# Making the first image's queries, keys and values beside the second image's Mamba tiles

## The chip, the cores and the metric

The kernel runs on one core of a Trainium2 chip. The metric is the time on the device in microseconds (us). Before the change it is 4571.91 us, the median of three runs (4563.61, 4571.91 and 4572.27); the execution that was profiled took 4562.89 us and its profile spans 4561.0 us. The core has five engines that work at the same time, each through its own instructions in their order: PE (matrix products), DVE (vector work), ACT (activation functions, also copies), POOL (general work, here elementwise products) and SP, which here only issues transfers (DMA).

## The reference

Two images of 256 channels by 4096 positions (64 x 64) pass through two layers, each added to its own input. Cut to what matters:

```
# layer 0, on groupnorm(x): a Mamba block and an MLP, per image
yn  = layernorm(y) * gamma + beta
xm, z = split(yn @ W_in.T)                     # 512 channels each
u   = silu(causal_conv4(xm) + conv_b)
dt  = softplus(W_dt @ (W_xp @ u)[:16] + b_dt)  # B, C: the other 2 x 16 rows
h   = exp(dt * A) * h + (dt * u) * B           # one step per position, 16 states per channel
ym  = (sum(h * C) + u * D) * silu(z)
y2  = ym @ W_out.T + yn
x   = x + gelu(y2 @ W1.T + b1) @ W2.T + b2 + y2

# layer 1, on groupnorm(x): attention, 8 heads of 32 channels over 4096 positions
q, k, v = split(groupnorm(x) @ qkv_w.T + qkv_b)
x   = x + softmax(q.T @ k / sqrt(32)) @ v
```

Layer 1 of an image needs the whole of layer 0 of that image, since its group norm takes means over all positions; it needs nothing of the other image.

## The kernel before

**Stages.** The program is `mamba_stage` for both images, then `attention_block` for image 0, then for image 1. Positions are cut into tiles of 512, so an image has 8 tiles and the Mamba stage 16, image 0 first.

**The Mamba stage.** A tile is worked in 32 steps: 4 groups of 128 channels times 4 groups of states times 2 halves. In each step ACT makes two decays `da` (L725), PE spreads a row of B over the partitions (`bn`, L418), POOL and DVE multiply it with dt * u (`dbu` and `bn`, L731), DVE runs two scans (L736) into a tile `h`, POOL multiplies `h` by C (L742), and PE sums over the states into `y` (L768). Around the steps of a tile lie its `front` (load, norms, convolution, softplus; POOL takes part with L587, L588 and L590) and its `back`: the product with W_out (L614), and the MLP, whose 8 blocks of hidden values go through PE, ACT's gelu (L639) and PE again (L650). Its end adds the input, takes statistics for layer 1's group norm (L660 and L661) and stores the tile to a scratch in memory (L664).

**What sets the order.** The order in each engine is not written by hand: every operation is added to a `Plan` with an engine, a due time counted in steps, a cost in us, what it reads and writes, and for transfers a time to land. `Plan.order` then runs these through in planned time and gives each engine the ready operation with the earliest due time; the result is the order in which instructions are issued, and the chip follows that order per engine whatever the real times are. So an instruction that waits holds all that stands behind it on its engine. For a transfer the planner counts mostly 0.8 us of SP and 2 to 5 us of landing (3.0 for stores of 512 KB). Buffers are rings of the same planner: `mm` has 3 PSUM banks for all products but `bn` and `y`, `bn` 2, `h` 5, `yn` 3, and `hid`, the 8 blocks of the MLP's hidden values, is one buffer (16 KB in each partition). A tile's MLP can only begin to fill it when the tile before has read it.

**Attention of an image.** `prepare` loads the weights w_qkv, takes the group norm's scales, and for each of 8 tiles loads x, normalises (L894), makes keys and queries (L904) as two halves each, a rounded high one (L914, ACT) and the rest (L915, DVE), stores both to memory (L918), makes values (L927, L934) into the buffer `v`, and loads keys back in the layout of the heads (L823). Then the main loop takes 512 slots of one block of 128 keys for 4 heads: logits on PE (L987), exponentials on ACT (L1000), products with v on PE (L1021) and sums of the exponentials on DVE and POOL (L1013, L1051 to L1054). In its first tiles it also stores `v` to memory, 128 transfers in all, for a fallback that only runs if a value has gone out of range.

Of the kernel before, what the change touches and what calls it, by code (L numbers as in the profile page):

```python
# [11 lines left out]
F32 = mybir.dt.float32  # L12
F32R = mybir.dt.float32r
AF = mybir.ActivationFunctionType
ALU = mybir.AluOpType
# [4 lines left out]
P = 128  # L20
T = 512
# [4 lines left out]
KG = HEADS * D // P  # L26
# [215 lines left out]
SWITCH = 6  # L242
HORIZON = 24


@with_exitstack
def mamba_stage(ctx, tc, xs, stats_out, consts, w, outs):

# [23 lines left out]
    KH = HID // P  # L272
# [8 lines left out]
    wp = ctx.enter_context(tc.tile_pool(name="l0w", bufs=1))  # L281
# [7 lines left out]
    mm = ring("mm", 3, pool=ps, free=True)  # L289
# [10 lines left out]
    r_hid, r_xb = ring("hid", 1, KH), ring("x_back", 1, KC)  # L300
# [3 lines left out]
    add = plan.add  # L304

    def image_tile(x, t):
        return x.rearrange("(k p) l -> p k l", p=P)[:, :, bass.ts(t, T)]


    stats_in = [wp.tile([P, KC, NT, nc.vector.BN_STATS_DIM], F32, name=f"stats_in{b}") for b in range(IMAGES)]  # L310
    stats_bufs = [Buf(parts=KC * NT, tile=s) for s in stats_in]

    def first(b, t, due):
        xt = Buf(r_h)
# [68 lines left out]
    for row in (0, LOW):  # L383
        rows = slice(row, row + R)
# [14 lines left out]
    late_buf = Buf()  # L399

    def load_late():
        for tile_, name in ((w_out, "W_outT"), (w_1, "W1T"), (w_2, "W2T")):
            nc.sync.dma_start(tile_, w[name].rearrange("(k p) f -> p k f", p=P))

# [5 lines left out]
    nc.vector.memset(halo, 0.0)  # L410
    state_buf = Buf(parts=IMAGES * KD * QUAD * NQ, tile=state)
    halo_buf = Buf(parts=IMAGES * KD, tile=halo)
    scales = wp.tile([P, IMAGES, KC, 2], F32, name="scales")
    scales_buf = Buf(parts=IMAGES * KC, tile=scales)

    def matmul(out, pairs):
        for i, (lhsT, rhs) in enumerate(pairs):
# [2 lines left out]
    def group_norm(b, k, due):  # L420

        s = Buf(r_gn)
        p1, p2 = Buf(mm), Buf(mm)
        out = scales_buf[b * KC + k]

        def aggregate():
            nc.vector.bn_aggr(s.tile[:, 0:2], stats_in[b][:, k, :, :].rearrange("p a s -> p (a s)"))

        def spread():


            nc.vector.tensor_copy(s.tile[:, 2:3], p1.tile[:, 0:1])
            nc.vector.tensor_sub(s.tile[:, 3:4], s.tile[:, 0:1], s.tile[:, 2:3])
            nc.vector.scalar_tensor_tensor(
                s.tile[:, 4:5], s.tile[:, 3:4], s.tile[:, 3:4], s.tile[:, 1:2], ALU.mult, ALU.add
            )

        def root():
            nc.scalar.activation(s.tile[:, 5:6], p2.tile[:, 0:1], AF.Ln, bias=eps_t)
# [12 lines left out]
        add("DVE", due, 0.2, shift, [s], [out])  # L452
# [8 lines left out]
    STEPS = KD * NQ * 2  # L461
# [142 lines left out]
    def back(i):  # L604

        b, t = divmod(i, NT)
        d = tiles[i]
        due = (i + 1) * STEPS + 3
        yn = d.yn
        for m in range(KC):  # L610
            po = Buf(mm)

            def project(k, po=po, m=m):
                nc.tensor.matmul(  # L614
                    po.tile, lhsT=w_out[:, k, bass.ts(m, P)], rhs=d.z[k].tile, start=(k == 0), stop=(k == KD - 1)
                )
# [12 lines left out]
        hid = Buf(r_hid, KH)  # L629
        xt = Buf(r_xb, KC)  # L630
        add("SP", due + 6, 0.8, lambda: nc.sync.dma_start(xt.tile, image_tile(xs[b], t)), [], [xt], lands=4.0)
        for f in range(KH):
            ph = Buf(mm)

            def up(f=f, ph=ph):
                matmul(ph.tile, [(w_1[:, c, bass.ts(f, P)], yn.tile[:, c, :]) for c in range(KC)])

            def gelu(f=f, ph=ph):
                nc.scalar.activation(hid.tile[:, f, :], ph.tile, AF.Gelu, bias=b_1[:, f : f + 1])  # L639

            add("PE", due + 5 + 1.5 * f, 1.9, up, [yn], [ph, hid] if f == 0 else [ph])
            add("ACT", due + 6 + 1.5 * f, 0.7, gelu, [ph], [hid[f]], ("gelu",))
        for m in range(KC):
            acc = Buf(mm)

            def down(f, acc=acc, m=m):
                if f == 0:
                    nc.tensor.matmul(acc.tile, lhsT=ident, rhs=yn.tile[:, m, :], start=True, stop=False)
                for f in (f, f + 1):
                    nc.tensor.matmul(  # L650
                        acc.tile, lhsT=w_2[:, f, bass.ts(m, P)], rhs=hid.tile[:, f, :], start=False, stop=(f == KH - 1)
                    )

            for f in range(0, KH, 2):
                reads = [hid, yn[m]] if f == 0 else [hid[f], hid[f + 1]]
                add("PE", due + 19 + 4 * m + f / 2, 2.7 if f == 0 else 1.8, lambda f=f, down=down: down(f), reads, [acc])

            def end(m=m, acc=acc):
                x = xt.tile[:, m, :]
                nc.vector.scalar_tensor_tensor(x, acc.tile, b_2[:, m : m + 1], x, ALU.add, ALU.add)  # L660
                nc.vector.bn_stats(stats_out[b][:, m, t, :], x)  # L661

            add("DVE", due + 24 + 4 * m, 1.45, end, [acc], [xt[m]])
        add("SP", due + 29, 0.8, lambda: nc.sync.dma_start(image_tile(outs[b], t), xt.tile), [xt], [], lands=3.0)  # L664


    class Step:
# [120 lines left out]
    for i, d in enumerate(tiles):  # L788
        d.z, d.b, d.c, d.dt_rep, d.dtu_rep = [], [], [], {}, {}
        if i + 1 < len(tiles):  # L790
            front(i + 1)
        for k in range(KD):
            gate(d, k, i * STEPS + 8 * k - 1)
            for g in range(NQ * 2):
                step(i * STEPS + k * NQ * 2 + g)
        back(i)
    with tc.manual_schedule():
        plan.issue()

# [27 lines left out]


@with_exitstack
def attention_block(ctx, tc, b, stats, consts, w, out, scratch, range_t):  # L830

# [4 lines left out]
    nc = tc.nc  # L836
    ident, gmat, _, eps_t = consts
# [113 lines left out]
                        load_keys(0, t - 1)  # L951
                load_keys(0, NT - 1)

    prepare()

    p1 = ctx.enter_context(tc.tile_pool(name=f"l1p1{b}", bufs=1))
    p3 = ctx.enter_context(tc.tile_pool(name=f"l1p3{b}", bufs=2))
# [133 lines left out]
    with tc.manual_schedule():  # L1091
        logits(0, 0)
        logits(0, 1)
        s = 0
        while s <= S or side.waiting:
            i, c = divmod(s, NC)
            if s < S:
                if c == 0:
                    tiles[i] = Slot()
                    load_queries(i + 1)  # L1100
                if i % NT == NT - 1 and i < KG * NT - 1 and c % (T // P) == 0:

                    load_keys(i // NT + 1, c * P // T)
                exponentials(s, 0)
                exponentials(s, 1)
            if 1 <= i <= KG:
                nc.sync.dma_start(scratch.v[b * KG + i - 1, :, c, :], v[:, c, (i - 1) * P : i * P])
            if 0 < s <= S:
                values(s - 1)
                if c == 0:  # L1110
                    side.start(side.now, finish(i - 1))
            side.run()
            logits(s + 1, 0)
            logits(s + 1, 1)
            if s < S:
                add_up(s)
            s += 1
# [100 lines left out]
def conv_preact_kernel(ctx: ExitStack, tc: tile.TileContext, x: bass.AP, w: dict, out: bass.AP):  # L1218
# [16 lines left out]
    scratch = Scratch(ctx.enter_context(tc.tile_pool(name="scratch", bufs=1, space=DRAM)), B * KG, L)  # L1235
    range_t = const.tile([P, 2, B * KG * NT], F32, name="range_t")
    stats1 = [const.tile([P, KC, NT, nc.vector.BN_STATS_DIM], F32, name=f"stats1{b}") for b in range(B)]
    mamba_stage(tc, [x[b] for b in range(B)], stats1, consts, w, [scratch.image(b) for b in range(B)])
    for b in range(B):
        attention_block(tc, b, stats1[b], consts, w, out[b], scratch, range_t)  # L1240
    flag = out_of_range(tc, range_t)
    with tc.If(flag > 0):
        attention_any_range(tc, consts, w, out, scratch)
# [51 lines left out]
```

## Time and profile before

| stage | from, us | to, us | what is seen |
|---|---|---|---|
| Mamba, steps of 16 tiles | start | 2024 | POOL 119.0 us of every 120, DVE 112, ACT 100, DMA 0.36 of its time |
| end of the last tile | 2024 | 2068 | PE nearly alone: W_out, the MLP |
| preparation of image 0 | 2068 | 2171 | PE 91 of 101 us, DMA 0.88, POOL 0 |
| attention of image 0 | 2171 | 3312 | PE, ACT, DVE and POOL all busy |
| preparation of image 1 | 3312 | 3413 | as for image 0 |
| attention of image 1 | 3413 | 4561 | as for image 0 |

| engine | busy us | share of the span |
|---|---|---|
| PE | 4266.7 | 94% |
| DVE | 3945.2 | 86% |
| POOL | 3816.1 | 84% |
| ACT | 3747.0 | 82% |

How to read it: busy time of the whole span mixes stages with different limits, so each stage has to be looked at by itself. PE's busy time counts matmuls that overlap from start to end, and an instruction can be counted busy while the next is already in the array. A row of the profile names the line, the engine, the tile that is written and the tiles that are read, the number of instructions, the busy time and the mean of one, and then the idle time of the engine just before them and what ended it. A line such as L418 is a helper for several products: there the tiles tell which.

### The profile page before, as it was taken

The numbers are of one execution on the slowest core, as the hardware profiler recorded it, in microseconds if no ns is written. First come the engines' busy times: TensorE is split into PE (matmuls) and PEld (weight loads), VectorE is DVE, ScalarE is ACT, GpSimd is POOL, SyncE is SP. The second block draws the span as 40 slices with busy tenths as digits, with TensorE's granted clock in tenths as the row PEclk, the third lists the DMA queues.
The fourth block names the chain that finished last, engine by engine and source line by source line (L and its number), as shares of the span: only waits on it lengthen the run. The fifth ranks groups of instructions, "written<-read, shape, count | busy, mean of one in ns | idle before, by whom it ended". The sixth has DMA issues, their size and how long they took to land. (4 is left out here: it accounts for less than half of the span.)

```text
span 4561.0 us, 53981 instructions
## 1 busy us (share of the span) xinstructions
PE 4266.7 (94%) x18530; PEld 1640.5 (36%) x18530; DVE 3945.2 (86%) x3340; ACT 3747.0 (82%) x4801; POOL 3816.1 (84%) x2251
## 2 busy tenths in 40 slices
PE   5889999999999999888999999999989999999998
PEld 2233333333333333324333333333343333333333
DVE  4999999999999999963789898898948898898988
ACT  4788888888888888751999999999829999999997
POOL 2999999999999999970788888888808888888887
PEclk9899999999999999989999999999999999999999
DMA  5233333333333333317220140101082101401000
GB/s 190 99 120 121 105 104 121 121 125 125 125 125 114 118 123 123 103 51 233 77 55 17 26 94 24 27 17 26 10 265 54 45 17 26 102 17 26 25 23 8
DMA packets 162315, 379.54 MB, mean 83 GB/s; under 512 B 23409, under 2 KB 41585, under 8 KB 153841
## 3 DMA queue, kind: packets, MB, share of 16 engines
q1 hardware_dynamic: 162032, 376.03, 26.9%
q8 instruction: 147, 2.41, 0.2%
q14 instruction: 136, 1.11, 0.1%
HBM read 282.64 MB, written 93.32 MB: 82 GB/s over the span
## 5 line engine op out<-in xcount | busy, mean ns | idle before, releaser
L1013 DVE TENSOR_REDUCE chunk<-chunk 128x1024 f32<-128x4096 f32 x288 | 1269.8, 4409 | 209.4 <-ACT chunk L1000 209.4
L1000 ACT ACTIVATE chunk<-s 128x1024 f32<-128x1024 f32 x992 | 1118.3, 1127 | 180.9 <-PE s L987 139.3
L1054 POOL TENSOR_TENSOR acc_p<-acc_p,e 128x1024 f32<-128x1024 f32 x480 | 1152.1, 2400 | 136.0 <-ACT e L1000 117.3
L987 PE MATMUL s<-q,k 128*128 128x512 f32 x4096 | 1224.8, 420 | 3.6 <-ACT chunk L1000 2.3
L742 POOL TENSOR_TENSOR h<-h,c 128x1024 f32<-128x1024 f32 x512 | 1205.1, 2367 | 14.1 <-ACT state L739 9.5
L1021 PE MATMUL po<-chunk,v 128*32 128x512 f32 x3968 | 1114.6, 640 | 0.0
L1021 PE MATMUL po<-e,v 128*32 128x512 f32 x4224 | 1079.1, 605 | 0.0
L1000 ACT ACTIVATE e<-s 128x1024 f32<-128x1024 f32 x1056 | 1071.0, 1017 | 7.6 <-PE s L987 7.2
L987 PEld LDWEIGHTS s<-q,k 128*128 128x128 f32 x4096 | 689.0, 188 | 1006.8 <-issue 910.8
L725 ACT ACTIVATE da<-dt_rep,neg_a 128x512 f32<-128x512 f32 x1024 | 692.2, 701 | 126.5 <-DVE h L736 105.0
L1052 POOL TENSOR_TENSOR acc_p<-acc_p,e 128x512 f32<-128x512 f32 x480 | 630.4, 1313 | 161.2 <-ACT e L1000 138.3
L736 DVE TENSOR_TENSOR_SCAN h<-da,state,dbu 128x512 f32<-128x512 f32 x512 | 649.9, 1274 | 81.2 <-POOL dbu L731 76.0
L736 DVE TENSOR_TENSOR_SCAN h<-da,state,bn 128x512 f32<-128x512 f32 x512 | 647.3, 1265 | 14.3 <-POOL dt L588 0.5
L731 POOL TENSOR_TENSOR dbu<-dtu_rep,b 128x512 f32<-128x512 f32 x384 | 486.9, 1279 | 11.7 <-DMA dtu_rep<-dtu_dram 11.7
L234 ACT ACT_TABLE_LOAD x336 | 431.1, 1283 | 6.6 <-PEq L1285 0.7
L768 PE MATMUL y<-h,sum 128*32 128x512 f32 x2048 | 381.4, 640 | 39.2 <-POOL h L742 38.7
L418 PE MATMUL bn<-proj,pick 112*128 112x512 f32 x512 | 304.1, 611 | 120.9 <-DVE h L736 120.4
L731 DVE TENSOR_TENSOR bn<-dtu_rep,bn 128x512 f32<-128x512 f32 x512 | 348.8, 681 | 27.4 <-DMA dtu_rep<-dtu_dram 14.3
L1051 DVE TENSOR_TENSOR acc<-acc,e 128x512 f32<-128x512 f32 x448 | 309.7, 691 | 24.1 <-ACT e L1000 14.0
L1045 POOL TENSOR_TENSOR acc_p<-e 128x1024 f32<-128x1024 f32 x32 | 76.8, 2401 | 273.2 <-ACT chunk L1000 110.4
L1021 PEld LDWEIGHTS po<-chunk,v 128*32 128x32 f32 x3968 | 142.9, 108 | 360.7 <-issue 349.6
L418 PE MATMUL mm<-yn,w_in 128*128 128x512 f32 x512 | 256.7, 627 | 12.5 <-ACT yn L507 8.6
(128 smaller groups left out, 4201.8 us busy)
## 6 DMA issues: line engine op xcount, KB each, us to landing
dt_rep<-dt_dram SPq DMA_DIRECT2D x128, 512.0 KB, 5.1
dtu_rep<-dtu_dram SPq DMA_DIRECT2D x128, 512.0 KB, 5.4
qk_dram<-halves SPq DMA_DIRECT2D x64, 512.0 KB, 5.9
q<-qk_dram SPq DMA_DIRECT2D x128, 256.0 KB, 4.8
k<-qk_dram SPq DMA_DIRECT2D x64, 512.0 KB, 7.6
b<-bc_dram SPq DMA_DIRECT2D x64, 256.0 KB, 3.0
c<-bc_dram SPq DMA_DIRECT2D x64, 256.0 KB, 4.1
dt_dram<-dt SPq DMA_DIRECT2D x64, 256.0 KB, 2.0
```

What stands on the lines that cost most here:

```text
L234: self.nc.scalar.preload_act_table_set(self.TABLES[task.table])
L418: nc.tensor.matmul(out, lhsT=lhsT, rhs=rhs, start=(i == 0), stop=(i == len(pairs) - 1))
L725: nc.scalar.activation(da[j].tile, dt.tile[:, j, :], AF.Exp, scale=scale)
L731: engine.tensor_mul(out.tile, dtu.tile[:, j, :], rows.tile)
L736: nc.vector.tensor_tensor_scan(h.tile[:, j, :], da[j].tile, dbu.tile, initial, ALU.mult, ALU.add)
L742: nc.gpsimd.tensor_tensor(h.tile, h.tile, rows_c.tile.unsqueeze(1).to_broadcast([P, 2, T]), ALU.mult)
L987: nc.tensor.matmul(ps[:, j, :], lhsT=keys[i // NT, kt][:, h, kj : kj + P], rhs=queries[i][:, h, :], start=True, stop=True)
L1000: nc.scalar.activation(e, todo[s].s[half], AF.Exp, scale=SCALE)
L1013: nc.vector.tensor_reduce(out, terms, AX.XY, ALU.add)
L1021: nc.tensor.matmul(tiles[i].po[h * D : (h + 1) * D, :], lhsT=v[:, c, g * P + h * D : g * P + (h + 1) * D], rhs=todo[s].e[h // 2][:, h % 2, :],
L1052: nc.gpsimd.tensor_add(acc_p[:, 1, :], acc_p[:, 1, :], eb[:, 1, :])
L1054: nc.gpsimd.tensor_add(acc_p, acc_p, eb)
```

## The change

The queries, keys and values of image 0 are made in the Mamba stage, in the eight tiles of image 1, by operations that go to the same planner. They need space for weights, input and results, and take it from `hid`: of its 8 blocks, 3 hold w_qkv (loaded anew for each tile), 2 the tile of x, 2 the halves, 1 the values. So `hid` is used in turn by a tile's MLP and by one tile's `qkv`. The tile t of image 0 is due 20 steps into tile 9 + t of the sixteen. The halves and the values are stored to the same scratch as before. `attention_block` for image 0 then has no `prepare`: it loads queries, keys and values from memory, and no longer stores the values itself. For image 1 nothing changes. The aim is to fill the time in which the stage before leaves engines free, and to let the first image's attention start without a stage of its own for the products.

The diff, cut to its core:

```diff
-    stats_bufs = [Buf(parts=KC * NT, tile=s) for s in stats_in]
+    stats_bufs = [Buf(parts=KC * NT, tile=s) for s in stats_in + stats_out]
...
     def load_late():
+        nc.sync.dma_start(b_qkv, w["qkv_b"].rearrange("(k p) -> p k", p=P))
...
-            add("PE", due + 5 + 1.5 * f, 1.9, up, [yn], [ph, hid] if f == 0 else [ph])
+            add("PE", due + 5 + 1.5 * f, 1.9, up, [yn], [ph, hid if f == 0 else hid[f]])
...
+    def qkv(b, t, due):
+        hid = Buf(r_hid, KH)
+        halves = [hid[5], hid[6]]
...
+        def load():
+            nc.sync.dma_start(flat(0, 3).rearrange("p (k f) -> p k f", k=KC), w["qkv_wT"].rearrange("(k p) f -> p k f", p=P))
+            nc.sync.dma_start(hid.tile[:, 3:5, :], image_tile(outs[b], t))
+        def norm(k):
+            x = hid.tile[:, 3 + k, :]
+            sc = scales[:, IMAGES + b, k, :]
+            nc.scalar.activation(x, x, AF.Identity, bias=sc[:, 0:1], scale=sc[:, 1:2])
+        add("SP", due, 1.6, load, [stored[b * NT + t]], [hid], lands=6.0)
...
+        for n, (i, m) in enumerate(((1, 0), (1, 1), (0, 0), (0, 1))):
+            pm = Buf(mm)
...
+            at = due + 3 + 2.2 * n
+            add("PE", at, 1.8, project, [hid[k] for k in range(5)], [pm, *halves])
+            add("ACT", at + 0.5, 0.7, high, [pm], [hid[5]])
+            add("DVE", at + 1, 0.7, low, [pm, hid[5]], [hid[6]])
+            add("SP", at + 1.5, 0.8, store, halves, [], lands=3.0)
+        for j in range(0, T // P, 2):
+            pv = Buf(mm)
...
+            at = due + 4 + 2.2 * j
+            add("PE", at, 1.8, project, [hid[k] for k in range(5)], [pv, hid[7]])
+            add("ACT", at + 0.5, 0.7, lambda pv=pv: nc.scalar.copy(hid.tile[:, 7, :], pv.tile), [pv], [hid[7]])
+            add("SP", at + 1, 1.6, store, [hid[7]], [], lands=3.0)
...
         back(i)
+        t = i + 1 - NT
+        if 0 <= t < NT:
+            if t == 0:
+                for k in range(KC):
+                    group_norm(IMAGES, k, (i + 1) * STEPS + QKV - 1)
+            qkv(0, t, (i + 1) * STEPS + QKV)
...
-    prepare()
+    def load_prepared():
+        def load_values(g, t):
+            cs = bass.ts(t, T // P)
+            nc.sync.dma_start(v[:, cs, g * P : (g + 1) * P], scratch.v[b * KG + g, :, cs, :])
+        with tc.manual_schedule():
+            load_queries(0)
+            for t in range(NT):
+                load_keys(0, t)
+                load_values(0, t)
+            for g in range(1, KG):
+                for t in range(NT):
+                    load_values(g, t)
+    load_prepared() if prepared else prepare()
...
-            if 1 <= i <= KG:
+            if 1 <= i <= KG and not prepared:
                 nc.sync.dma_start(scratch.v[b * KG + i - 1, :, c, :], v[:, c, (i - 1) * P : i * P])
```

`project` is the product of a block of weights with the normalised tile, `high` the rounded half (ACT), `low` the rest (DVE, from PSUM and `high`), `store` the transfer of both halves, or of the values, to memory.

More of the change, by code (lines that the diff above doesn't have):

```diff
@@ L243, with mamba_stage @@
 HORIZON = 24
+QKV = 20
 @with_exitstack
[L247 removed]
+def mamba_stage(ctx, tc, xs, stats_out, consts, w, outs, scratch):
     nc = tc.nc
@@ L412, in mamba_stage @@
     halo_buf = Buf(parts=IMAGES * KD, tile=halo)
-    scales = wp.tile([P, IMAGES, KC, 2], F32, name="scales")
-    scales_buf = Buf(parts=IMAGES * KC, tile=scales)
+    scales = wp.tile([P, IMAGES + 1, KC, 2], F32, name="scales")
+    scales_buf = Buf(parts=(IMAGES + 1) * KC, tile=scales)
+    stored = [Buf() for _ in range(IMAGES * NT)]
+    b_qkv = wp.tile([P, 3 * KC], F32, name="b_qkv")
     def matmul(out, pairs):
@@ L426, in aggregate @@
         def aggregate():
-            nc.vector.bn_aggr(s.tile[:, 0:2], stats_in[b][:, k, :, :].rearrange("p a s -> p (a s)"))
+            nc.vector.bn_aggr(s.tile[:, 0:2], (stats_in + stats_out)[b][:, k, :, :].rearrange("p a s -> p (a s)"))
         def spread():
@@ L661, in end @@
                 nc.vector.bn_stats(stats_out[b][:, m, t, :], x)
-            add("DVE", due + 24 + 4 * m, 1.45, end, [acc], [xt[m]])
-        add("SP", due + 29, 0.8, lambda: nc.sync.dma_start(image_tile(outs[b], t), xt.tile), [xt], [], lands=3.0)
+            add("DVE", due + 24 + 4 * m, 1.45, end, [acc], [xt[m], stats_bufs[IMAGES + b][m * NT + t]])
+        store = lambda: nc.sync.dma_start(image_tile(outs[b], t), xt.tile)
+        add("SP", due + 29, 0.8, store, [xt], [stored[b * NT + t]], lands=3.0)
@@ new lines, in qkv, with flat, weights, project @@
+    def qkv(b, t, due):
+        hid = Buf(r_hid, KH)
+        halves = [hid[5], hid[6]]
+        def flat(a, n):
+            return hid.tile[:, a : a + n, :].rearrange("p a t -> p (a t)")
+        def weights(c, at, n):
+            return flat(0, 3)[:, c * 3 * C + at : c * 3 * C + at + n]
+        def load():
[7 more added lines that the diff above has]
+        for k in range(KC):
+            add("ACT", due + 2, 0.75, lambda k=k: norm(k), [hid[3 + k], scales_buf[(IMAGES + b) * KC + k]], [hid[3 + k]])
+        for n, (i, m) in enumerate(((1, 0), (1, 1), (0, 0), (0, 1))):
+            pm = Buf(mm)
+            def project(i=i, m=m, pm=pm):
+                matmul(pm.tile, [(weights(c, i * C + m * P, P), hid.tile[:, 3 + c, :]) for c in range(KC)])
+            def high(i=i, m=m, pm=pm):
+                bias = b_qkv[:, i * KC + m : i * KC + m + 1]
+                nc.scalar.activation(hid.tile[:, 5, :].bitcast(F32R), pm.tile, AF.Identity, bias=bias)
+            def low(i=i, m=m, pm=pm):
+                bias = b_qkv[:, i * KC + m : i * KC + m + 1]
+                nc.vector.scalar_tensor_tensor(
+                    hid.tile[:, 6, :].bitcast(F32R), pm.tile, bias, hid.tile[:, 5, :], ALU.add, ALU.subtract
+                )
+            def store(i=i, m=m):
+                nc.sync.dma_start(
+                    scratch.qk[b * KG + m, i, t].rearrange("s c h t -> (c h) s t"), hid.tile[:, 5:7, :]
+                )
+            at = due + 3 + 2.2 * n
[5 more added lines that the diff above has]
+            pv = Buf(mm)
+            def project(j=j, pv=pv):
+                for n in range(2):
+                    rows = bass.ts(j + n, P)
+                    matmul(pv.tile[:, bass.ts(n, C)], [(hid.tile[:, 3 + c, rows], weights(c, 2 * C, C)) for c in range(KC)])
+            def store(j=j):
+                for g in range(KG):
+                    cs = t * (T // P) + j
+                    nc.sync.dma_start(
+                        scratch.v[b * KG + g, :, cs : cs + 2, :],
+                        hid.tile[:, 7, :].rearrange("p (n g c) -> p g n c", n=2, g=KG)[:, g],
+                    )
+            at = due + 4 + 2.2 * j
+            add("PE", at, 1.8, project, [hid[k] for k in range(5)], [pv, hid[7]])
+            add("ACT", at + 0.5, 0.7, lambda pv=pv: nc.scalar.copy(hid.tile[:, 7, :], pv.tile), [pv], [hid[7]])
+            add("SP", at + 1, 1.6, store, [hid[7]], [], lands=3.0)
@@ L796, in mamba_stage @@
         back(i)
+        t = i + 1 - NT
+        if 0 <= t < NT:
+            if t == 0:
+                for k in range(KC):
+                    group_norm(IMAGES, k, (i + 1) * STEPS + QKV - 1)
+            qkv(0, t, (i + 1) * STEPS + QKV)
     with tc.manual_schedule():
@@ L829, in attention_block @@
 @with_exitstack
-def attention_block(ctx, tc, b, stats, consts, w, out, scratch, range_t):
+def attention_block(ctx, tc, b, stats, consts, w, out, scratch, range_t, prepared):
     nc = tc.nc
@@ L1237, in conv_preact_kernel @@
     stats1 = [const.tile([P, KC, NT, nc.vector.BN_STATS_DIM], F32, name=f"stats1{b}") for b in range(B)]
-    mamba_stage(tc, [x[b] for b in range(B)], stats1, consts, w, [scratch.image(b) for b in range(B)])
+    mamba_stage(tc, [x[b] for b in range(B)], stats1, consts, w, [scratch.image(b) for b in range(B)], scratch)
     for b in range(B):
-        attention_block(tc, b, stats1[b], consts, w, out[b], scratch, range_t)
+        attention_block(tc, b, stats1[b], consts, w, out[b], scratch, range_t, b == 0)
     flag = out_of_range(tc, range_t)
```

## The prediction

> **What bounds the kernel now.** I read the page's 40 slices first, to part the run into stages, and then each stage by its own table of windows.
>
> ```profile
> ## 2 busy tenths in 40 slices
> PE   5889999999999999888999999999989999999998
> ...
> POOL 2999999999999999970788888888808888888887
> ...
> DMA  5233333333333333317220140101082101401000
> ```
>
> The first 18 slices (114 us each) are the Mamba stage. POOL then falls to 0 in one slice while DMA jumps to 7, again in slice 29: these are the two preparations, in which queries, keys and values are made. The windows table gives the share of each stage (columns: stretch, its length, then busy us of PE, PEld, DVE, ACT, POOL with counts, granted clock, DMA share, GB/s).
>
> ```profile
> 1380.00:1500.00 120.00, 111.13 (x339) 41.61 (x338) 112.37 (x123) 100.66 (x167) 119.00 (x76) 0.97 0.36 119
> 1500.00:1620.00 120.00, 110.14 (x340) 41.30 (x339) 112.39 (x123) 100.40 (x167) 118.99 (x77) 0.99 0.36 119
> ...
> 2070.00:2171.00 101.00, 91.25 (x266) 52.67 (x266) 40.86 (x64) 24.39 (x35) 0.00 (x0) 0.90 0.88 270
> ```
>
> A Mamba tile takes 120 us (these windows repeat to within 0.1 us on POOL, and the 76 to 77 POOL instructions in one are a tile's 32 + 24 + 12 + 8). POOL works 119.0 of the 120; DVE has 7.6 us free, ACT 19.5, PE 9.5 by a busy time that counts overlapping matmuls as long. In the preparation (last row) no engine but PE is near busy and DMA runs at 0.88 of its time, 270 GB/s. How Mamba's own waits look, in the table of waits between 1100 and 2000 us (total, times, longest):
>
> ```profile
> DVE h L736 <- POOL dbu L731: 40.4, 45, 2.8
> ...
> DVE bn L731 <- DMA dtu_rep<-dtu_dram: 5.7, 5, 2.8
> ...
> POOL h L742 <- ACT state L739: 4.8, 7, 0.7
> DVE bn L731 <- PE bn L418: 4.8, 10, 1.4
> ...
> POOL dbu L731 <- DMA dtu_rep<-dtu_dram: 1.3, 1, 1.3
> ```
>
> POOL waits 6.1 us in 900; most of DVE's waiting (40.4) is for POOL. So POOL sets Mamba's pace, DVE follows within one step, and what PE waits for is mostly the scan that frees its bank. Last, the hand-over, in the order of time of ACT, SP and DVE (start, length, instruction, idle time before it):
>
> ```profile
> 2051.11 0.69 ACT L639 ACTIVATE hid<-mm,b 128x512 f32<-128x512 f32 x1 [1.03 <-PE mm L418]
> ...
> 2083.93 0.69 ACT L914 ACTIVATE halves<-s,b_qkv 128x512 fp32r<-128x512 f32 x1 [9.15 <-PE s L904]
> ...
> 2171.27 1.07 ACT L1000 ACTIVATE chunk<-s 128x1024 f32<-128x1024 f32 x1 [0.91 <-PE s L987]
> ```
>
> ```profile
> 2067.35 0.69 DVE L661 BATCH_NORM_STATS2 stats<-x_back 128x6 f32<-128x512 f32 x1
> ```
>
> Mamba's last arithmetic ends at 2068.0 and the first exponential of attention starts at 2171.3. Those 103.3 us are what the change goes for. The image-1 preparation (near 3312 to 3413) stays.
>
> **What the Trainium skill says.** Trace analysis ("Perfetto Trace Analysis", Identifying the Most-Contended Engine) holds matmul busy time to be a bad measure of PE and wants weight-load busy instead: here 41 of 120 us, so PE has room that the 110 hides; the trace agrees, since PE waits 51.7 us in 900 for the scans. "SBUF — State Buffer" (Who interferes with whom) says that a DVE instruction with two SBUF inputs contends with a reading GpSimd one, one with a single SBUF input doesn't: the added `low` reads PSUM and one SBUF tile, so I charge POOL nothing; no run here shows it apart. "ScalarE: Activation LUTs" (What ACT_TABLE_LOAD costs) gives 1283 ns a load, the trace's mean exactly (L234, 1283); the order of issue of the changed program has 341 loads in its list where before had 340, so the added Identity and copy steps bring one. "DMA: Bandwidth & Descriptors" (Anatomy of one DMA) gives 2.0 us + bytes/436e3, 3.2 us for 512 KB; the trace has 4.0 for such a load (yn) and 7.0 for such a store beside Mamba's bursts (x_back), so the trace is used for the stores.
>
> **The change, part by part.**
>
> *Removed: the preparation.* 2068.0 to 2171.3, 103.3 us, all of it on the path.
>
> *Added in its place: loads.* The queue issues b_qkv, 4 pieces of q, 2 of k, 1 of v. From the last store at 2067.3 the trace has b_qkv at 2067.8, and the next load only at 2070.3, when that store had landed (2.8 us, the shortest in its row); the keys' load has the same kind of wait. The q and k pieces then take about 0.56 us each to issue and 4.8 us (the page's median for q) to 7.6 (for k) to land: the first logits at 2071.5 + 5 to 8, with 1 us for the matmul. First exponential 9 to 14 us after Mamba's end; I take 11. Then k and v come at 1.25 MB per four slots of 2.18 us; at the 270 GB/s of the preparation that is 4.6 us of every 8.7, so attention isn't starved. Gain: 103.3 - 11 = 92.
>
> *Added to eight tiles of image 1.* Per tile, on ACT 2 norms at 0.71 (row L507), 4 `high` at 0.69 (L914), 2 copies at 0.57 (L555): 5.3 us of 19.5 free. On DVE 4 `low` at 0.75 (L915): 3.0 of 7.6 free. On PE 8 matmuls of 512 columns at 0.44 (32 of them in 14.1 us at the end of Mamba) and 8 of 256 at 0.23: 5.3 us. POOL nothing. DMA 0.75 MB of weights, 0.5 of x, 2.0 of halves, 0.5 of values: 3.75 MB on 14.3 (119 GB/s for 120 us), so the share goes from 0.36 to about 0.45. By sums all of it lies beside POOL's 119 us: the floor is 0.
>
> *The waits that come with it.* `halves` is one buffer, so each projection on PE waits until the store of the one before has landed. A link is project 1.1, high 0.7, low 0.75, queueing 0.5, store 2.8 (least) to 7.0 (x_back's median): 6 to 10 us, and the planner counts 3.0 us for landing. With three links, PE can stand up to 3 x 4 = 12 us a tile at a wait that the planner didn't foresee; queued behind it are the broadcasts `bn` that DVE needs and the sums `y` that free `h`. PE is one to two steps (3.75 us each) ahead, and DVE has 4.6 us left per tile to catch up, so of 12 us, less 3.75, less 4.6, about 4 would reach POOL (6 if the lead is half a step), and of 3 or 4 us nothing. The SP queue has such waits in order too, with dt_rep loads behind. In the issue order of the changed program tile after tile repeats, the first softplus comes 3 steps earlier than before and the second 3 steps later, still 7 steps ahead of its use, so I don't see the front starve. Bounds 0 and 6 us a tile; I take 2, for eight tiles 16.
>
> *The MLP's buffer.* It is now held by two users in turn. In the issue order the ups start 2 steps later and end 5 later; what they make is needed by no scan, only by the tile's own store. Nothing, hidden under POOL's 119 us.
>
> *The last tile.* The issue order puts the fourth projection of tile 7 between the two halves of W_out, and the third before the last `y`. Both wait for stores. DVE has two `low` (1.5 us) before its last scan, PE stands for a store about twice, gelu for the last one: before, gelu began 15.3 us after the last scan. Between 2 and 10 us; I take 5.
>
> *At nothing:* 128 stores of v leave attention's queue (1.7 us each, beside exponentials); b_qkv's load goes into the late weights; the group norm's small instructions come once, in one tile, beside POOL.
>
> Sum: -92 + 16 + 5 = -71. 4571.9 - 71 = 4501 us.
>
> **The rivals.**
> 1. *All of it hides in image 1.* DVE and ACT sums speak for it, the single `halves` buffer against: -103.3 + 9 + 2 = -92, 4480.
> 2. *PE becomes the bound while it stands at store waits.* 5 to 6 us a tile and 10 at the end: -92 + 45 + 10 = -37, 4535. For it: x_back's 7.0 us landing, bn already just in time in places (10 waits of PE's bn, 4.8 us). Against: PE's own waits for scans (51.7 us in 900) are room that its delays can use up first.
> 3. *Slower than before.* The MLP's buffer, held by qkv for some 35 us and by the MLP for 45 or more, pushes the fronts out, or the SP queue stands so long that dt_rep loads come late: it takes (92 - 5)/8 = 11 us a tile to lose everything, and at 13 it is slower: -92 + 104 + 5 = +17, 4589. For it: DVE already waits 5.7 us for dtu_rep loads, and x_back's load waits for its store (45.8 us in 7 waits of the SP queue). Against: the rest of the queue has whole gaps of 10 to 30 us in a tile.
>
> **How the numbers follow.** Forecast (within about 15 us of 4501) 0.58, rival 1 0.13, rival 2 0.21, rival 3 with all that ends over 4563 0.08. The range goes from rival 1 less the 4 us by which the median could stand lower (4476) to rival 2 with its last bounds, 6 us a tile and a first exponential after 14 us (-89 + 48 + 10 = -31, 4541); the 8 of rival 3 and some 10 at the edges stay outside. Faster 0.92, same 0.02, slower 0.06, with rival 3 parted between same and slower.
>
> **What would show it.** In the changed profile: no stretch of POOL at 0 between Mamba and image 0's attention but some 55 us (tail and load), instead of 147 (2024 to 2171); first exponential 9 to 14 us after the last stats; tiles of image 0 at 120 us, of image 1 at 122, with POOL 119 us in each; ACT up by 5.3, DVE by 3.0 per tile; PE waits for qk_dram stores as a new row. Wrong it would be made by tiles of image 1 over 127 us, by DVE waiting for dtu_rep over 3 us a tile, by keys that starve the first 70 us of attention, or by a tail over 10 us longer.

## The result and the profile after

| | before | after |
|---|---|---|
| median, us | 4570.91 (4 runs, 4563.61 to 4572.27) | 4531.6 (4 runs, 4528.19 to 4536.84) |
| ratio | | 0.9918, 95% interval 0.9901 to 0.9935 |

The change gains about 39 us, 0.8% (the two profiled executions, 4562.9 and 4532.6, lie 30.3 apart, which is what the ledger below parts). The forecast was 4501, the range 4476 to 4541, so the time lies inside, at the place of rival 2 (4535). The forecast was a gain of 71 us, and a little more than half of it came. Whether the reason is rival 2's is what the rest is about.

The 40 slices of the changed kernel, from its page (113 us each):

```profile
## 2 busy tenths in 40 slices
PE   5799989999899999988999999999899999999998
...
POOL 2999999999999999994888888888708888888887
...
DMA  5233333333443344444311040110091100401100
```

POOL's empty slice after the Mamba stage is gone; only the second preparation is left (the 30th slice). DMA stands mostly at 4 in place of 3 from the 11th slice on, where image 1's tiles begin. Two windows in image 1, and the first 57 us after Mamba's end (stretch, length, busy us of PE, of PEld, which is PE's loading of weights, of DVE, ACT and POOL, granted clock, DMA share, GB/s):

```profile
1420.00:1540.00 120.00, 113.45 (x353) 45.28 (x354) 108.31 (x120) 98.88 (x162) 112.64 (x74) 0.97 0.45 147
1540.00:1660.00 120.00, 110.13 (x341) 44.49 (x339) 107.64 (x119) 97.99 (x165) 111.59 (x72) 0.99 0.47 152
2123.00:2180.00 57.00, 44.54 (x234) 17.87 (x235) 28.90 (x12) 41.37 (x41) 35.50 (x18) 0.88 1.05 226
```

POOL is no longer at 119 of 120 but at 112: something else sets the pace. The hand-over, from the timeline between 2120 and 2140 us (start, length, engine, where SPq is the queue of SP, and in brackets the idle time before it):

```profile
2120.60 0.69 DVE L668 BATCH_NORM_STATS2 stats<-x_back 128x6 f32<-128x512 f32 x1
...
2121.53 2.40 SPq L910 DMA_DIRECT2D q<-qk_dram  x4
2124.11 1.17 SPq L907 DMA_DIRECT2D k<-qk_dram  x2
...
2134.61 2.90 PE L1086 MATMUL s<-q,k 128*128 128x512 f32 x6 [14.83 <-DMA v<-v_dram]
2135.95 1.28 ACT L1099 ACT_TABLE_LOAD   x1 [30.89 <-PE s L1086]
2137.24 1.07 ACT L1099 ACTIVATE chunk<-s 128x1024 f32<-128x1024 f32 x1
```

The last statistics end at 2121.3, the first exponential starts at 2137.2: 15.9 us where there were 103.3. From such places the ledger of the span (4561.0 to 4530.8):

| | before | after | difference |
|---|---|---|---|
| last scan ends | 2023.8 | 2077.8 | +54.0 |
| of it from image 1 (counted from tile 9's store of `bc`) | 871.7 | 922.0 | +50.4 |
| tail: last scan to last statistics | 44.2 | 43.5 | -0.7 |
| last statistics to first exponential | 103.2 | 15.9 | -87.3 |
| the rest, both attentions | 2389.7 | 2393.6 | +3.9 |
| sum (the span: -30.2) | | | -30.1 |

The tile of image 1, from one store of `bc` (one per tile, L528 before, L535 after) to the next over six tiles, is 128.6 us in place of 120.7; in image 0 it is still 120.8. So eight tiles took back more than half of what the shorter start gave. (Before, one of the six tiles took 122.1, and their mean is 120.9. The expectations below, from another stretch, say 128.8.) "D" below is the row "from image 1": from the start of tile 9's store to the start of the last scan, 7.2 tiles long. Its two ends, before and then after:

```profile
1150.90 0.32 SPq L528 DMA_DIRECT2D bc_dram<-bc  x1
2022.55 1.26 DVE L736 TENSOR_TENSOR_SCAN h<-da,state,bn 128x512 f32<-128x512 f32 x1
```

```profile
1154.52 0.32 SPq L535 DMA_DIRECT2D bc_dram<-bc  x1
2076.54 1.27 DVE L814 TENSOR_TENSOR_SCAN h<-da,state,bn 128x512 f32<-128x512 f32 x1
```

The other 3.6 us of the +54.0 lie ahead of tile 9's store. In the traces of the other runs below this store starts anywhere between 1150.6 and 1156.0 us (one run, of tiles of 140 us, apart), so these 3.6 us are put down to no cause.

What the waits between 1100 and 2000 us say, in the changed kernel (total, times, longest), POOL's first and then ACT's:

```profile
POOL h L820 <- ACT state L817: 19.1, 22, 3.1
POOL dbu L809 <- DMA dtu_rep<-dtu_dram: 16.4, 10, 2.5
```

```profile
ACT state L817 <- DVE h L814: 26.7, 45, 2.0
ACT hid L705 <- DMA qk_dram<-hid: 22.1, 10, 4.0
ACT da L803 <- DVE h L814: 21.9, 28, 1.6
ACT yn L479 <- DMA yn<-in_x: 21.2, 5, 4.9
ACT da L803 <- DMA dt_rep<-dt_dram: 18.3, 13, 2.8
```

The wait for the stores of the halves is there, but ACT stands in it (writing the next high half), not PE. Late loads show too: before, `yn` cost ACT 0.9 us, `dt_rep` 3.4, and `dtu_rep` cost POOL 1.3. This table suggests three culprits: stores, traffic, and DVE and ACT being fuller. All three were tested first, and none was the main one. What DVE's added work costs by itself was not taken apart from PE's.

### The profile page after: what moved, and what is told of

It is laid out like the page before. It is cut to its first block, busy times and chain, and to the rows that moved or that the text cites. A ratio compares the mean times of both kernels' runs of the same rounds, so it can differ in the third digit from the quotient of the medians.

```text
span 4530.8 us, 53988 instructions
## 1 busy us (share of the span) xinstructions
PE 4248.6 (94%) x18530; PEld 1638.8 (36%) x18530; DVE 3931.0 (87%) x3316; ACT 3762.3 (83%) x4836; POOL 3821.2 (84%) x2251
## 5 line engine op out<-in xcount | busy, mean ns | idle before, releaser
L425 PE MATMUL bn<-proj,pick 112*128 112x512 f32 x512 | 309.2, 617 | 111.3 <-DVE h L814 111.1
L846 PE MATMUL y<-h,sum 128*32 128x512 f32 x2048 | 358.8, 638 | 24.4 <-POOL h L820 24.0
L425 PE MATMUL mm<-xm,taps 128*128 128x512 f32 x512 | 237.1, 606 | 11.1 <-POOL xm L561 8.7
```

Source lines behind the costliest of these rows:

```text
L425: nc.tensor.matmul(out, lhsT=lhsT, rhs=rhs, start=(i == 0), stop=(i == len(pairs) - 1))
```

## The experiments

Besides the whole time, every run was read by D and by the tile (six stores of `bc`). The runs with one execution were beside runs of the kernel before on the same chip (4572.6 us in the first set, 4567.0 in the second, 4567.9 in the third). Each D is that of one traced execution, and how far it scatters was not measured; differences of 2 to 4 us are not to be leaned on.

### First set: order, work, transfers, stores

The theories: A, ACT stands for the landing of the halves' stores; B, the added transfers make the Mamba loads late; C, the planned order alone leaves too little time; and a fourth, which the expectations call theory D (not the measure D), the added instructions fill ACT and DVE. "Order only" plans every added operation and emits none (load, norms, `low`, copies and stores as the two shown); image 0 keeps its preparation, here and in the next two:

```
-            add("PE", at, 1.8, project, [hid[k] for k in range(5)], [pm, *halves])
-            add("ACT", at + 0.5, 0.7, high, [pm], [hid[5]])
+            add("PE", at, 1.8, none, [hid[k] for k in range(5)], [pm, *halves])
+            add("ACT", at + 0.5, 0.7, none, [pm], [hid[5]])
...
-        attention_block(tc, b, stats1[b], consts, w, out[b], scratch, range_t, b == 0)
+        attention_block(tc, b, stats1[b], consts, w, out[b], scratch, range_t, False)
```

> The planner sees all of qkv's operations, but none of them is issued; image 0 makes its queries, keys and values in its own preparation as before. What is left of the change in the Mamba stage is the order of the other instructions alone. Measured by the time from one store of B and C to the next in image 1, which is 120.7 us before and 128.8 us after. Theory A (ACT stands for the landing of qk stores): 120.7 to 121.5. Theory B (the added transfers make the loads of dt, dt u and yn land late): the same. Theory C (the new order leaves too little time between producer and consumer, whatever is added): 127 or more. Theory D (the added instructions themselves fill ACT and DVE): 120.7 to 121.5.

Measured: tile 126.6, D 907.2 (+35.5), whole 4603.3. Two thirds of the loss are there with not one instruction added: just under the 127 of theory C, and far from the 121.5 of the others.

The second run emits all but the stores (`none` for the two `store`):

> As the change, but the halves and the values are not stored, and image 0 makes them again in its own preparation. Weights and x are still loaded, all products, norms and halves are computed. Tile time in image 1 (120.7 before, 128.8 after). A: 121 to 123, since nothing is left to wait for. B: two thirds of the added bytes are gone, so 122 to 124. C: 127 or more. D: 127 or more.

Measured: tile 127.2, D 911.1 (+39.4), whole 4609.6. So the work adds 3.9 in this order, and the stores with their waits the last 11.0.

The third emits the loads and stores, from blocks that the load fills, and none of the norms, products and copies:

```
-                    scratch.qk[b * KG + m, i, t].rearrange("s c h t -> (c h) s t"), hid.tile[:, 5:7, :]
+                    scratch.qk[b * KG + m, i, t].rearrange("s c h t -> (c h) s t"), hid.tile[:, 3:5, :]
```

> The added transfers alone: weights and x are loaded and blocks of the same sizes are stored to the same places, but from the loaded x, so that a store waits for that load and for nothing that is computed; no norm, product, half or copy is issued, and image 0 makes its own in its preparation. Tile time in image 1. A: 121 to 122, since ACT waits for none of it. B: 125 to 129. C: 127 or more. D: 121.

Measured: tile 126.4, D 905.9 (+34.2), whole 4606.9: as order only. The 3.75 MB a tile add nothing to what that order costs, so B falls, though 126.4 lies in its range. The waits for late `yn` and `dt_rep` that the table above shows belong to the order: order only, with no byte added, has them too (ACT 18.8 and 18.1 us between 1150 and 2000).

The fourth is the full change, with the planner told that the stores, those of v too, land late:

```
-            add("SP", at + 1.5, 0.8, store, halves, [], lands=3.0)
+            add("SP", at + 1.5, 0.8, store, halves, [], lands=7.0)
...
```

> The whole change, with one number altered: the planner counts 7.0 us instead of 3.0 for the landing of a store of halves or values, which in the changed kernel took 5.1 and 6.4 us. A: ACT's waits for the landing (22.1 us in 900) go to under 5 us and the tile time falls by 2 to 4 us, to 125 to 127, the whole run by 15 to 30 us. B, C, D: the tile time stays within 1.5 us of 128.8.

Measured: tile 129.5, D 922.0, whole 4540.0. ACT's wait for the stores fell from 22.1 us to 8.4 (theory A had said under 5), but nothing was gained. Other waits took its place: POOL stood 30.9 us for ACT's copies of the scan state, where it had stood 19.1. From ACT's table and from POOL's, between 1100 and 2000 us:

```profile
ACT hid L706 <- DMA qk_dram<-hid: 8.4, 3, 3.0
```

```profile
POOL h L821 <- ACT state L818: 30.9, 30, 6.1
```

So planning 7.0 us for the stores brings no gain. What they cost in the order of the changed kernel remains the 11.0 us of the second run.

### Second set: what in the order

A new theory, C': the planner books PE too high, so that its order makes room that nobody needs. It rested on a price of 0.9 us for a product booked at 1.8.

Order only, but with PE and DVE booked at nothing for the added steps (`1.8` and `0.7` to `0.05`):

> The order-only kernel (image 0's queries, keys and values still made in their own preparation; in the eight tiles of image 1 the added loads, products, copies and stores are planned but issue nothing), with the planner told that the added PE and DVE steps cost 0.05 us each in place of 1.8 and 0.7. Theory C' (the order is spread because the planner books PE and DVE as full: six products at 1.8 us bring PE's booked sum per tile from about 113 to 124 us, while the chip takes 0.9): tiles of image 1 fall from 126.6 to 121-123 us, last scan about 890 us or less after the store of bc of tile 9 (order-only 907, before 872). Rival (the sharing of the MLP's buffer by two users sets the order, whatever the products cost): 126 us, 903-910.

Measured: tile 122.8, D 885.7 (+14.0), whole 4585.2. So of the 35.5 us of the order, 21.5 are the room that is kept for PE and DVE; how they part between the two was not tested.

Order only, with the added steps on a planned buffer of their own (`Buf(r_own, KH)` for `Buf(r_hid, KH)`):

> The same order-only kernel with the planned queries, keys and values on a buffer of their own (planned only, it takes no memory) in place of the MLP's, at the costs booked by the changed kernel. Theory C' (booked PE and DVE sums): stays near 126 us a tile, last scan 903-912 us after the store of bc of tile 9. Rival (sharing the MLP's buffer delays the MLP, and with it the release of yn and the next fronts): 120.7-122 us, 872-882.

Measured: tile 126.2, D 905.2 (+33.5), whole 4603.0. Sharing the MLP's buffer is worth 2 us of this order, no more.

So far C' held. Then the full change with the costs of most of PE's products about halved (not those of `bn`, `y` and the product for `dt`) and two of DVE's lowered (scan 1.27 to 1.2, multiplication 0.7 to 0.6):

```
-        add("PE", due - 14, 3.6, project, d.u, [pp, proj, bc])
+        add("PE", due - 14, 1.8, project, d.u, [pp, proj, bc])
...
```

> The full change, with the planner's costs set to what the profile shows: a 512-column product of four 0.95 in place of 1.8, the pairs and fours alike halved, the scan 1.2 in place of 1.27, the multiplication by B 0.6 in place of 0.7. Theory C': the booked sums of PE and DVE fall below POOL's, the order comes close to that of before, tiles of image 1 take 121-124 us in place of 128.8 and the whole 4485-4505 us. Rival 'ACT stands for the stores' (order without part): tiles stay at 127-129 and the whole at 4525-4535. If both hold, 125-126 and 4505-4515.

Measured: 4779.9 us, ratio 1.0464 (1.0447 to 1.0481), tiles of about 140 us even in image 0, where nothing was added. DVE's and PE's waits between 1160 and 1900 us show who was late:

```profile
DVE bn L809 <- PE bn L425: 54.7, 28, 6.5
```

```profile
PE bn L425 <- DVE h L814: 86.0, 57, 4.3
```

DVE stands for the broadcasts of PE, and PE for the scans of DVE. The reading is that with its products booked at half, the planner puts too many of them ahead of the broadcasts that the scans need; PE's and DVE's costs were not altered one by one, and the granted clock was lower too (0.949 in the mean, where the other runs have 0.972 to 0.98), so what each has of the 4.6% is not shown. The full change with only the six added products halved (`1.8` to `0.9`):

> The full change with only the six added products booked at 0.9 us in place of 1.8 (nothing else differs from the changed kernel). Theory C': booked PE sum falls from about 124 to 118 us, tiles of image 1 take about 126 us, whole run 4508-4522. Rival (booked cost of the added products is not the cause): 128.8 and 4528-4535.

Measured: tile 128.2, D 920.8, whole 4531.9. No difference; C' falls in the full kernel, and the rows of PE show that its price was wrong. Its groups by shape in the changed kernel, between 1154 and 1926 us (six tiles):

```profile
L425 PE MATMUL mm<-hid 128*128 128x512 f32 x96 | 47.5, 618 | 0.0
L425 PE MATMUL mm<-hid 128*128 128x256 f32 x96 | 23.2, 384 | 0.0
```

That is 16 and 16 a tile. The code has 8 and 8: four products of keys and queries, and values for four row blocks, each over two channel blocks. Each of these f32 matmul instructions is two records in this trace. Those of the broadcasts `bn`, whose operands the code makes in the rounded format fp32r, are one: 32 a tile in the code, and 193 records in the six tiles.

```profile
L425 PE MATMUL bn<-proj,pick 112*128 112x512 f32 x193 | 123.7, 646 | 33.2 <-DVE h L814 33.2
```

The MLP's first half shows the two again, in the kernel before, at Mamba's end where PE is alone: 8 blocks of two instructions are 16, and the line has 32 in 14.1 us.

```profile
2036.99 14.09 PE L418 MATMUL mm<-yn,w 128*128 128x512 f32 x32
```

So 0.44 us is the price of a record, 0.88 that of an instruction, and 1.76 that of a product of two: the planner's 1.8 was right, and the prediction's 5.3 us a tile should have been 10.7. PE ran nothing for about 10 us of a tile.

### Third set: PE's work by itself

Theory P: PE's own work is the bound. All else as in the changed kernel, with half the work in the added products (shown; so for the values), and with double (the list taken twice):

```
-  matmul(pm.tile, [(weights(c, i * C + m * P, P), hid.tile[:, 3 + c, :]) for c in range(KC)])
+  matmul(pm.tile, [(weights(c, i * C + m * P, P), hid.tile[:, 3 + c, :]) for c in range(1)])
```

> The full change with each of its products left half done: only the first of the two channel blocks is multiplied (so image 0's queries, keys and values are wrong), all else, the planned order too, as in the changed kernel. Theory P (formed after the four runs before: PE itself is the bound; each matmul of the added products is two records of PE, so they are 16 of 512 columns at 0.44 us and 16 of 256 at 0.23, 10.7 us a tile and not the 5.3 of the prediction, where PE has 10 us free in 120.7): PE's work falls by 5.3 us a tile, tiles of image 1 take 123.5-125.5 us in place of 128.8, the whole run 4495-4512. Rival (the planned order, or ACT's waits for the stores, set the pace whatever PE works): 128-129 and 4528-4536.

Measured: tile 128.1, D 918.8, whole 4531.6. P was wrong here: 5 us less of PE's work bring 0.5 us a tile (3.2 of D).

> The full change with each of its products made twice over into the same sum (so image 0's queries, keys and values come out doubled), all else, the planned order too, as in the changed kernel. Theory P: PE's work rises by 10.7 us a tile, tiles of image 1 take 136-140 us in place of 128.8, the whole run 4590-4620. Rival (order or store waits set the pace): 129-132 and 4531-4560.

Measured: tile 136.1, D 977.1 (+105.4), whole 4590.4, as P had it, at the low end of its ranges. Of the 55.0 us of D over the changed kernel, 45 lie in the six tiles and 10 in the last one.

The last of the set leaves before's order nearly alone and gives PE the work in each tile of image 1 without telling the planner:

```
+    def added_products(due):
...
+            matmul(pm.tile, [(w_out[:, c, 0:P], w_1[:, c, 0:T]) for c in range(KC)])
+            add("PE", due + 3 + 2.2 * n, 0.05, project, [late_buf], [pm])
```

> The kernel before (image 0's preparation stays) with nothing added but the PE work of the new products: in each tile of image 1 six products of the same shapes, on weights that lie in SBUF, whose results nobody reads; no loads, copies or stores. The planner is told they cost 0.05 us, so that it leaves no room for them and spreads nothing. Theory P: tiles of image 1 grow by 6-9 us (126.5-130 in place of 120.7), the last scan comes 920-945 us after the store of bc of tile 9 (before 872), the whole run 4620-4645. Rival (PE has room, as the prediction had it; the order and the other engines' additions did it): 120.7-122.5, 872-886, 4572-4588.

Measured: tile 125.5, D 903.5 (+31.8), whole 4599.6. Less than P had in all three (4.8 us a tile in place of 6 to 9), but far from "PE has room". The products stand here in an order that was made as if they cost nothing, so what they cost in a better one is not shown.

What the two sets say together is in the sums of the six windows from 1180 to 1900 us. One line each for before, after, order only, half, double, products in before's order, and order only without room for PE and DVE:

```profile
sum 720.00, PE 661.55 PEld 248.76 DVE 673.09 ACT 601.38 POOL 712.65; mean PE 110.26 PEld 41.46 DVE 112.18 ACT 100.23 POOL 118.78
```

```profile
sum 720.00, PE 668.41 PEld 265.81 DVE 651.25 ACT 595.13 POOL 672.61; mean PE 111.40 PEld 44.30 DVE 108.54 ACT 99.19 POOL 112.10
```

```profile
sum 720.00, PE 637.74 PEld 236.64 DVE 647.09 ACT 582.12 POOL 684.39; mean PE 106.29 PEld 39.44 DVE 107.85 ACT 97.02 POOL 114.07
```

```profile
sum 720.00, PE 645.31 PEld 248.22 DVE 654.31 ACT 596.71 POOL 675.49; mean PE 107.55 PEld 41.37 DVE 109.05 ACT 99.45 POOL 112.58
```

```profile
sum 720.00, PE 675.11 PEld 283.09 DVE 617.42 ACT 561.91 POOL 635.52; mean PE 112.52 PEld 47.18 DVE 102.90 ACT 93.65 POOL 105.92
```

```profile
sum 720.00, PE 684.31 PEld 271.65 DVE 648.73 ACT 591.55 POOL 688.98; mean PE 114.05 PEld 45.27 DVE 108.12 ACT 98.59 POOL 114.83
```

```profile
sum 720.00, PE 652.49 PEld 245.95 DVE 667.13 ACT 601.40 POOL 700.75; mean PE 108.75 PEld 40.99 DVE 111.19 ACT 100.23 POOL 116.79
```

The mean per 120 us, times the tile over 120, is PE's busy time in a tile; what is left of the tile is its idle time:

| run | tile | PE busy | PE idle | D over before |
|---|---|---|---|---|
| before | 120.7 | 110.9 | 9.8 | |
| order without room for PE and DVE, no work | 122.8 | 111.3 | 11.5 | +14.0 |
| products alone in before's order | 125.5 | 119.3 | 6.2 | +31.8 |
| order with room, no work | 126.6 | 112.1 | 14.5 | +35.5 |
| full, half of the products | 128.1 | 114.8 | 13.3 | +47.2 |
| the changed kernel | 128.6 | 119.4 | 9.2 | +50.4 |
| full, products doubled | 136.1 | 127.6 | 8.5 | +105.4 |

PE idles 6 to 10 us a tile, in waits for scans, for POOL's `h` and for `yn`, wherever its work fills the order it is given. (The run without stores, not in the table, has 8.8.) Where the order keeps room and the work, or half of it, is missing, it idles 13 to 15 and the tile hardly shortens. Where the work exceeds the room (double: +8.2 us busy on 128.6), the tile grows almost by as much (+7.5). No run takes away half of the products and the room for them together, which would test this from the other side.

### Last run: the full change without the room

Theory R joins these: the order costs the room that it keeps; without room, the products overrun. The edit is that of the fifth run, on the full change.

> The full change, with the planner told that its PE and DVE steps (six products, four low halves a tile) cost 0.05 us each in place of 1.8 and 0.7, so that its order leaves no room for them. Theory R (the order costs what room it makes, 5.9 us a tile with the work absent and 8.1 with it; without room the order costs 2.0 and the products overrun by 4.8, as in the two runs that had each alone): tiles of image 1 take 126-127.5 us in place of 128.8, whole run 4505-4522, a ratio to before of 0.986-0.990 where the changed kernel has 0.992. Rival S (the planner's room is what the work needs; an order without it stands still at its waits): 129-133 and 4532-4565. Rival T (PE's work hides in gaps): 122-124 and 4480-4495.

Measured: tile 126.7 as R said, but D 922.2 (+50.6) and the whole 4534.1 us, ratio 0.9919 (0.9905 to 0.9933), the same as the changed kernel. PE idled 7.8 us a tile. The 2 us that each of six tiles gained were lost in the last one: from its store of `bc` to the start of the last scan 161.9 us, against 150.4 in the changed kernel. R's parts add up (14.0 for the order and 31.8 for the products make 45.8 of 50.6), but its forecast of a faster run failed, and the whole lies in rival S's range, the tile not: without room or with it, the whole comes to the same. No version here beats the changed kernel.

## Why the prediction was right in the number and not in the reason

The number is right by luck. The range went up to 4541 for the sake of rival 2, in which PE stands at store waits; PE's table of waits from 1160 to 1900 us has none of these, and the forecast of 4501 itself is 31 us off. The prediction named tiles of image 1 over 127 us as a sign that it is wrong, and they took 128.6.

*Removed preparation, and loads in its place:* right in kind. 103.3 was read from the trace of before and holds (103.2 in the ledger). The start took 15.9 us in place of 11: no 2.8 us wait for the last store came, but the keys landed only in time for logits 10.5 us after their issue (2124.1 to 2134.6; 7.6 was counted), 1.3 us went into the first logits, and 1.28 us for the exponential's table was left out. The gain was 87.3 and not 92.

*The term that failed:* "On PE 8 matmuls of 512 columns at 0.44 [...] and 8 of 256 at 0.23: 5.3 us." Instructions were counted in the code and priced by a row that counts records, two to an instruction. It is 16 and 16, 10.7 us by the same prices; PE's busy time rose by 8.5 us a tile. With it falls the sentence drawn from it, "By sums all of it lies beside POOL's 119 us: the floor is 0": 110.9 + 8.5 is 119.4, so that PE and POOL would both have to work 99% of a 120.7 us tile while they wait for one another in fixed orders. Image 1 paid 50.4 us where 16 were forecast. The products alone, without the rest of the change, cost 31.8, and the order with room for them, without the products, 35.5; the two are not a sum, since the one stands for the other.

*"So PE has room that the 110 hides."* This came from the Trainium skill, "Perfetto Trace Analysis" (Identifying the Most-Contended Engine), which judges PE's headroom by MFU (the share of the peak arithmetic) and weight-load busy time, and not by matmul busy time. The prediction used the weight loads alone. In this case the measurement decides against that use: weight loads went from 41.5 to 44.3 us of 120 while PE's added work cost the time. Nearer to the truth were the 9.8 us of a tile in which PE ran nothing, and even of these not all could be used: the products alone lengthened the tile by 4.8.

*The store waits:* near in size, wrong in place. ACT stands, not PE; in the planned order the stores are worth 11.0 us of D, 1.5 us a tile where 2 was taken. But that is no gain to be had by itself: with ACT's wait cut to 8.4 us by planning, the time did not fall.

*The MLP's buffer:* "Nothing" was nearly right (2 us of D). *Issue order:* "I don't see the front starve" looked for the wrong thing; the order costs 35.5 us before any work is in it, and 21.5 of them are the room for PE's and DVE's work as the planner books it.

*The last tile:* 5 us were forecast, -0.7 came, as the tail is PE's own chain: W_out starts 3.7 us after the last scan in place of 4.6, and the fourth product takes 1.9 us between its halves. *Attention:* 3.9 us more. Of it 4.2 lie in image 1's preparation between its first and last high half (87.0 to 91.2 us), whose code is unchanged; image 0's attention was not starved (1126.4 to 1124.8 us from first to last exponential). The prediction has 128 stores of v leave attention's queue; these are the stores of both images, and 64 left.

*Rival 2* had the time (4535) and the engine, with the wrong cause: PE does not stand at stores, it works. Its parts were off both ways: 45 us for the eight tiles where 50.4 came, and 10 at the end where -0.7 came.

*Open:* why an order without room for PE and DVE still costs 14.0 us, with nothing emitted; ACT's and SP's booked steps are left, and were not taken out one by one. What lengthens the last tile by 11.5 us in the last run. And whether another order would let PE's added work cost less than it does here.

## What to carry to other kernels

Take price and count from the same place: if a row counts records, count records, and check it on a stretch where the code tells how many there are. The time in which an engine runs nothing in the stage, not its weight loads, bounds the room for added work, and not all of it can be used. Here POOL stood at 99% and PE at 92%, and filling PE cost from more than half to nearly all of what it added: 4.8 us a tile for 8.4 us of busy time (products alone), 7.9 for 8.5 (the changed kernel), 7.5 for 8.2 more (double). When a static order makes a kernel slower, running the order with the work taken out, and the work without the order, shows whether the two losses are one: here they were 35.5 and 31.8, and 50.4 together.

## What was not expected of the hardware

The stores and loads of 3.75 MB a tile (DMA share 0.36 to 0.46) cost nothing measurable by themselves (D +34.2 with them, +35.5 without). Nor are they the main reason why `yn` lands late: its 512 KB took 4.0 us before and 7.3 in the changed kernel, but 6.4 already in the order-only run, which adds no transfer to these tiles. At the start of attention, with DMA busy all of the time (1.05 in the window), 512 KB of keys took 16.4 us in the median from issue to landing and 256 KB of values 13.4, where the prediction counted 7.6 for the keys. The first piece of keys took 7.7 us, the third 11.7 and the fifth 15.4, each issued behind the others. And altering the planner's costs for PE's products and two of DVE's steps made the whole 4.6% slower, with the same instructions: so much rests on the costs that a fixed order is made from.
